# A graph layer by gathers: single rows given up for wider steps, and the waiting fillers computed by shifted sums and minima

## The chip, the cores and the metric

The kernel runs on one core of one Trainium2 chip. The metric is the device time of one execution in microseconds (us), as the median of several runs; lower is better. The engines of a core work side by side, each through its own list of instructions: PE multiplies matrices (its weight loads are shown apart, as PEld), DVE (VectorE) and ACT (ScalarE) work element by element, POOL (GpSimd) here does little else than issue gathers, and SP (SyncE) issues DMAs. A DMA moves data between memory and the core's on-chip buffers without any of them.

## The reference

N = 50000 nodes have D = 128 features each, and there are E = 1,650,000 edges (src, dst, type 0 or 1), sorted by dst. Every node has one edge to itself among them. The edges' messages are summed per destination, then a residual and a normalization follow:

```
msg = where(edge_type == 0, x[src] @ W_data.T + b_data, x[src] @ W_control.T + b_control)
agg = segment_sum(msg, dst)
out = layernorm(x + relu(agg + x @ W_self.T + b_self))
```

Since the message is linear in x[src], the kernel first sums the rows x[src] for each destination and type, and applies the two weight matrices to the sums. The heavy part is reading 1.6 million rows of 512 bytes at addresses that the data gives.

## The kernel before, in words

**Blocks and steps.** The sorted edges are cut into NBLK = 514 blocks of Q = 2 steps. A step has R = 12 columns of 128 edges, one edge in each of the 128 partitions, and in addition S = 24 edges that are fetched as single rows and F = 46 *fillers*, of which below. A block so takes up to 3212 edges in the order of their destinations and covers at most B = 112 destinations, a step at most W = 60. The first and the last block (`plain`) have neither single rows nor fillers; the last has RCH = 19 columns.

**Gathers.** For each column of 128 edges POOL issues one indirect DMA (L536) that fetches 128 rows of x into a tile `y`, by the addresses in `idx` (or `sdt`, the loaded list itself, for the last block, and `idx0` for the first). Gathers come in passes of PASS = 6, one tile `y` per pass; there are SLOTS = 10 such tiles, so POOL can be at most ten passes ahead of the products that read them. PE waits for a pass by a semaphore (L543).

**Products.** DVE compares each edge's column number (its destination relative to the step's first, plus W where the type is 1) with 0 to 2W - 1, which gives a one-hot matrix `oh` (L467), and counts the edges per destination (`cnt`, L475). For each column PE multiplies: the gathered rows as weights, the one-hot as the moving side, accumulated over the step in `acc` (L555); the single rows follow as one more product (L561), the counts as two (L564). In f32 each product shows as two loads and two matmuls in the trace. DVE adds a step's `acc` to the block's `sums` at the place of the step (`add`, L569). In the next block's turn PE applies the weights (`layer`, L586 to L590), DVE computes the residual and the moments (L596 to L603), ACT the root (L612), DVE the result (L618, L621), and SP stores it (L626).

**Single rows.** `offsets` (L490, DVE) turns source numbers into byte offsets, and `single_rows` (L496 to L513) has SP and ACT load them into registers and issue one DMA of 512 bytes for each, 12 per step on each of the two queues. PE waits for them in `rows_fetched` (L515 to L520).

**Self edges and fillers.** A node's edge to itself needs no gather, because x of the block's own nodes is there in any case (`window`, L438, by SP; `positions`, L453). Such an edge leaves a free place among the gathered columns, and a later edge, a *filler*, takes it. For each group of GB = 10 blocks, `columns` (L261) ranks the free places with matmuls (L284 to L287, `rank`), checks the order of the edges, packs source and column number into one number (L253), and follows, step by step, how many fillers are still waiting for a place: a chain of 20 additions with a lower bound of zero (L322 to L324, `late`), of which at most LATE = 10 may wait at once; FX = LATE + F. For each block, `spread` (L340, PE) puts the list of its fillers on all partitions, and `fill` (L349, DVE) finds the filler of each free place (L358 to L368), makes the gather's addresses `idx` (L369) and notes which self edge was left out (L373 to L378). `left_out_columns` (L384, PE), `left_out_matrix` (L392, DVE), `left_out_numbers` (L400, L403, PE) and `left_out_rows` (L409, DVE) make of it what is added to the sums instead (`begin_sums`, L571).

**Order.** The order is written by hand, and each engine keeps to it. One iteration of the loop (L682 to L735) is one block: loads for later blocks, `spread` for one or two later blocks (L690 lets the lists get up to RAHEAD = 5 blocks ahead, two blocks per iteration at most), the last `add` of the block before, `begin_sums`, `onehot` and `counts` two blocks ahead; then the four passes, with `fill` after the first, the layer of the block before after the second, `columns` of the next group after the third pass of the group's second block (L725), and the root and the stores after the fourth. Before the loop (L661 to L679) stand `columns(0)`, the lists of blocks 1 and 2 and the first one-hots. The block numbers that SP and DVE read as addresses (`base_i`, `at_i`) are computed ahead of `columns(0)` (L205 to L223). In the last block `find_bad` (L628) collects the checks; a kernel for general data (`general`) would run if they failed, and it doesn't with these data.

Of the kernel before, what the change touches and what calls it, by code (L numbers as in the profile page):

```python
# [21 lines left out]
ACT = mybir.EngineType.Activation  # L22
# [23 lines left out]
LOADS = 1  # L46
BEGIN = (0, -(-Q * TURNS[0] // 4) * 4)
X = BEGIN[1] + -(-Q * TURNS[1] // 4) * 4
R1 = R + 1
# [4 lines left out]
BE = CE + Q * (F + S)  # L54
# [27 lines left out]
GS = GB * Q  # L82
SPAN = 8
# [14 lines left out]
def straight(ctx, tc, c, x, x_t, edges_t, edges_f, src_x, dst_first, first_p, out):  # L98
# [62 lines left out]
    row_of = keep.tile([GB, GB], BF16, name="row_of")  # L161
    nc.vector.tensor_copy(row_of, c["ident"][:GB, :GB])
# [7 lines left out]
    one_g = {}  # L170

    def load_edges(g):
        t = eds.tile([1, GB * X], I32, name="one_g")
        nc.sync.dma_start(t, src_x[None, g * GB * X:(g + 1) * GB * X])
        one_g[g] = t
# [28 lines left out]
    nc.vector.tensor_tensor(begin_p, begin_p, base_p, op=ALU.add)  # L204
    wide = keep.tile([1, WG, SPAN], F32, name="wide")  # L205
    bases_f = keep.tile([1, WG * SPAN], F32, name="bases_f")
    nc.vector.memset(bases_f, float(N - B))
    nc.vector.tensor_copy(bases_f[:, :NBLK], base[0:1, :NBLK, 0])
    first_of_span = bases_f.rearrange("o (w s) -> o w s", s=SPAN)
    nc.vector.tensor_scalar(wide, first_of_span[:, :, 0:1].to_broadcast([1, WG, SPAN]), float(N - WIDE), None, op0=ALU.min)  # L210
    within = keep.tile([1, WG, SPAN], F32, name="within")
    nc.vector.tensor_tensor(within, first_of_span, wide, op=ALU.subtract)
    at_i = keep.tile([1, WG * SPAN, 4], I32, name="at_i")
    nc.vector.tensor_copy(at_i[:, :NBLK, :Q], begin[0:1, :NBLK, :])
    nc.vector.tensor_scalar(at_i[:, :, 3], within.rearrange("o w s -> o (w s)"), 0.0, float(WIDE - B), op0=ALU.max, op1=ALU.min)
    nc.vector.tensor_tensor(begin, begin, base.to_broadcast([P, BL, Q]), op=ALU.add)
    base_i = keep.tile([1, WG, 2 * SPAN], I32, name="base_i")
    nc.vector.tensor_scalar(base_i[:, :, 0], wide[:, :, 0], 4.0, None, op0=ALU.mult)
    nc.vector.tensor_scalar(base_i[:, :, 1:1 + SPAN], first_of_span, float(ROW), None, op0=ALU.mult)
    shift = keep.tile([1, NBLK], F32, name="shift")  # L220
    nc.vector.memset(shift, 0.0)
    nc.vector.tensor_tensor(shift[:, 1:], base[0:1, 1:NBLK, 0], base[0:1, :NBLK - 1, 0], op=ALU.subtract)
    nc.vector.tensor_scalar(at_i[:, :NBLK, 2], shift, 0.0, float(B), op0=ALU.max, op1=ALU.min)  # L223


# [27 lines left out]
    def packed(src, col):  # L253

        lim = eds.tile(list(col.shape), F32, name="lim", bufs=1)
        nc.vector.tensor_scalar(lim, col, 0.0, float(COLS - 1), op0=ALU.max, op1=ALU.min)
# [4 lines left out]
    def columns(g):  # L261
# [16 lines left out]
        h = eds.tile([P, GB, Q, R1], BF16, name="h_loop", bufs=1)  # L278
# [3 lines left out]
        rank = ps_r.tile([P, GB * Q, R1], F32, name="rank")  # L282
# [6 lines left out]
        col, rel = columns_of(a["d"], a["t"], first_of, "")  # L289
        check(a["d"], rel, [stats[:, 0, m, g:g + 1] for m in range(2)], "")  # L290
        col_f, rel_f = columns_of(a["df"], a["tf"], first_of_f, "_f")
# [5 lines left out]
        with nc.allow_low_precision(reason="whole numbers below 256 times a power of two"):  # L297
            nc.vector.tensor_scalar(v_f[:, 0, :], col_f, 0.0, float(COLS - 1), op0=ALU.max, op1=ALU.min)
            lo = eds.tile([GB, Q * FX], F32, name="lo", bufs=1)
# [30 lines left out]
        if n < GS and g > 0:  # L330
            nc.vector.memset(late[:, n + 1:], 0.0)
# [745 lines left out]
```

## Time and profile before

| what | us |
| --- | --- |
| median of 3 runs | 17994.12 |
| the 3 runs | 17983.56 to 17994.94 |
| the profiled execution | 18008.86 |
| its span (first to last instruction) | 18006.8 |
| mean granted TensorE clock, share of full speed | 0.54 |

The span is what the rows of the profile cover. A row of the page's fifth part, or of the view by lines, names a line of the kernel, the engine, the operation, the tiles out<-in with their shapes, the count, then after the bar the busy time in us, the mean of one in ns, and the idle time of the engine just before them with what ended most of it: an engine and its operation, "issue" when the engine waited for nothing that the profile shows, or "remote" for a releaser that the profile doesn't name. A row of the timeline gives the start, the duration, engine, line and operation, the count of equal instructions in a row, and in brackets the idle time before and its releaser. The table by stretches gives for a stretch of the span its length and each engine's busy time with its count in the order PE, PEld, DVE, ACT, POOL, then the granted clock, the mean busy share of the DMA engines and GB/s. The view of a line by source gives name, count and the shortest, middle and longest duration in ns.

### The profile page before, as it was taken

The page shows a single profiled execution, that of the slowest core. Times are in us where ns is not written, and L with a number is a line of the kernel's source. Part 1 is how long each engine was busy: PE and PEld are TensorE (multiplying, and loading weights), DVE is VectorE, ACT ScalarE, POOL GpSimd, SP SyncE. Part 2 cuts the span into 40 slices and gives each one's busy share as a digit, 9 for nine tenths or more (in the row PEclk, how much of TensorE's full clock was granted, in tenths as well). Part 3 has the DMA queues.
Part 4 walks back from the last instruction along what each step waited for, and adds up shares of the span by engine and source line. Part 5 has one row for each costly group of instructions (what it writes and reads, how often), then busy time and mean ns, then how long its engine had stood idle before and what let it go on. Part 6 is the DMA issues. An engine that isn't in the chain of part 4 may idle for free.

```text
span 18006.8 us, 165600 instructions
## 1 busy us (share of the span) xinstructions
PE 8608.7 (48%) x37659; PEld 7345.2 (41%) x37660; DVE 12374.8 (69%) x15212; ACT 79.2 (0%) x263; POOL 11686.9 (65%) x12341
## 2 busy tenths in 40 slices
PE   3444444444444444444444444444444444444444
PEld 3344443444344444444444444444444444444444
DVE  7676676676666666666766766676676676667665
ACT  0000000000000000000000000000000000000000
POOL 6666666666666666666666666666666666666666
PEclk6555555555555555555555555555555555555555
DMA  1111111111111111111111111111111111111111
GB/s 52 51 50 51 52 50 51 52 50 51 50 52 51 50 52 50 51 51 51 51 50 52 51 50 51 51 51 51 51 51 50 51 52 50 51 52 50 51 50 48
DMA packets 529272, 913.91 MB, mean 51 GB/s; under 512 B 232762, under 2 KB 315875, under 8 KB 528274
## 3 DMA queue, kind: packets, MB, share of 16 engines
q0 software_dynamic: 394592, 808.89, 15.7%
q1 hardware_dynamic: 108668, 87.80, 1.7%
q10 hardware_dynamic: 25014, 6.54, 0.2%
q8 instruction: 306, 5.01, 0.1%
q14 instruction: 692, 5.67, 0.1%
HBM read 872.82 MB, written 29.47 MB: 50 GB/s over the span
## 4 chain that ended last, share of the span: by engine, by line
DVE 51%; another core or an unknown queue 28%; issue 13%; PE 7%; DVEq 0%; ACTq 0%; ACT 0%
DVE cnt L475 14%; DVE oh L467 8%; PE acc L555 5%; DVE m L358 4%; DVE v_new L365 4%; DVE new L361 4%; DVE old L374 4%; DVE sums L569 2%; DVE late L323 1%; DVE z L392 1%; DVE h L597 1%; DVE st L599 1%; DVE xT L461 1%; DVE h L596 1%
## 5 line engine op out<-in xcount | busy, mean ns | idle before, releaser
L536 POOL DMA_INDIRECT y<-in_x,idx x12312 | 11667.4, 948 | 6272.6 <-issue 3435.2
L555 PEld LDWEIGHTS acc<-oh,y 128*128 128x128 f32 x24662 | 5375.0, 315 | 8665.3 <-issue 8100.0
L555 PE MATMUL acc<-oh,y 128*128 128x120 f32 x24662 | 6002.7, 413 | 3679.8 <-issue 3675.4
L569 DVE TENSOR_TENSOR sums<-acc,sums 128x180 f32 x1028 | 350.0, 340 | 4142.8 <-remote 3960.0
L475 DVE TENSOR_REDUCE cnt<-oh 128x240 bf16<-128x3120 f32 x514 | 3008.2, 5852 | 17.9
L384 PE MATMUL small<-ones_b,by 128*112 128x1 bf16 x512 | 83.5, 164 | 4632.6 <-issue 3934.5
L467 DVE TENSOR_TENSOR oh<-col,small 128x3120 f32<-128x3120 f32 x514 | 1740.8, 3387 | 117.3 <-remote 95.1
L377 DVE TENSOR_REDUCE by<-old 128x112 bf16<-128x1456 f32 x512 | 1427.3, 2788 | 17.4
L358 DVE TENSOR_TENSOR m<-rk,small 128x1456 f32<-128x1456 f32 x512 | 855.7, 1671 | 17.4
L361 DVE TENSOR_TENSOR new<-m,small 128x1456 f32<-128x1456 f32 x512 | 855.2, 1670 | 17.5
L365 DVE TENSOR_REDUCE v_new<-new 128x26 f32<-128x1456 f32 x512 | 855.0, 1670 | 17.5
L374 DVE TENSOR_TENSOR old<-m,small 128x1456 f32<-128x1456 f32 x512 | 852.5, 1665 | 0.0
L561 PE MATMUL acc<-oh,yx 24*128 24x120 f32 x2048 | 758.6, 466 | 61.6 <-issue 61.6
L590 PE MATMUL po<-wmsgT,sums 128*112 128x128 f32 x2056 | 612.8, 453 | 5.5 <-issue 5.5
L561 PEld LDWEIGHTS acc<-oh,yx 24*128 24x128 f32 x2048 | 486.9, 292 | 293.0 <-issue 281.7
L596 DVE COPY h<-po 112x128 f32<-112x128 f32 x514 | 144.8, 282 | 537.1 <-remote 451.3
L590 PEld LDWEIGHTS po<-wmsgT,sums 128*112 128x112 f32 x2056 | 448.4, 297 | 130.7 <-issue 130.0
L347 PE MATMUL small<-v_f,row_of 10*128 10x112 bf16 x1536 | 218.2, 272 | 563.8 <-DVE at L391 168.6
L588 PE MATMUL po<-bias,sums 3*112 3x128 f32 x1028 | 391.5, 482 | 0.2 <-DVE sums L569 0.2
L347 PEld LDWEIGHTS <-row_of 10*128 10x128 bf16 x1536 | 121.7, 112 | 599.5 <-issue 562.2
L587 PE MATMUL po<-wselfT,xT 128*112 128x128 f32 x1028 | 324.9, 420 | 0.0
L564 PE MATMUL acc<-cnt,to_row 128*128 128x60 bf16 x2056 | 281.2, 227 | 13.8 <-issue 13.7
(141 smaller groups left out, 4709.2 us busy)
## 6 DMA issues: line engine op xcount, KB each, us to landing
y<-in_x,idx POOLq DMA_INDIRECT x12312
yx<-in_x SPq DMA_DIRECT2D x12288, 0.5 KB
yx<-in_x ACTq DMA_DIRECT2D x12288, 0.5 KB
xw<-in_x_t SPq DMA_DIRECT2D x65, 448.0 KB
out<-o SPq DMA_DIRECT2D x514, 56.0 KB
sdt<-in_edges_t SPq DMA_DIRECT2D x52, 390.0 KB
one_g<-in_src_x SPq DMA_DIRECT2D x52, 1.9 KB
sdt_f<-in_edges_f SPq DMA_DIRECT2D x52, 13.1 KB
```

The lines of the kernel that those rows point to most:

```text
L358: nc.vector.tensor_tensor(m, rk_g[g][:, i, :, None].to_broadcast([P, C1, FX]), rank_no_ps[:, None, :].to_broadcast([P, C1, FX]), op=ALU.is ...
L361: nc.vector.tensor_tensor(new.rearrange("p (q r) f -> p q r f", r=R1), m.rearrange("p (q r) f -> p q r f", r=R1), vf.rearrange("p (q f) -> ...
L365: nc.vector.tensor_reduce(v, new, AX.X, ALU.add)
L374: nc.vector.tensor_tensor(old, m, cb[:, :, None].to_broadcast([P, C1, FX]), op=ALU.mult)
L377: nc.vector.tensor_reduce(by, old.rearrange("p (q r) f -> p q f r", r=R1), AX.X, ALU.add)
L467: nc.vector.tensor_tensor(oh, col_g[g][:, i, :, None].to_broadcast([P, C1, 2 * W]), num_ps[:, None, :].to_broadcast([P, C1, 2 * W]), op=AL ...
L475: nc.vector.tensor_reduce(cnt, ohs[b].rearrange("p (q r) w -> p q w r", r=R1), AX.X, ALU.add)
L536: copy = nc.gpsimd.indirect_dma_start(out=y[:r, k % PASS, :].bitcast(U8), out_offset=None, in_=x_rows, in_offset=bass.IndirectOffsetOnAxis ...
L555: nc.tensor.matmul(acc[:, :2, :].rearrange("p t w -> p (t w)"), y[:r, k % PASS, :], ohs[b][:r, column(k), :], start=k == of_step[0], stop= ...
L561: nc.tensor.matmul(acc[:, :2, :].rearrange("p t w -> p (t w)"), ys[b][:, q, :], ohs[b][:S, q * R1 + R, :], start=False, stop=True)
L569: nc.vector.tensor_tensor(part, accs.pop((b, q)), part, op=ALU.add)
L590: nc.tensor.matmul(po, a[:, t, :B], c["wmsgT"][:, t * D:(t + 1) * D], start=False, stop=t == 1)
```

## The change

Six things are changed together.

1. **No single rows.** `offsets`, `single_rows`, `rows_fetched`, their tiles, their semaphores and the product L561 go. In their place a step has R = 14 gathers instead of 12, in passes of 7 instead of 6, F = 53 fillers instead of 46, W = 64 and B = 124. A block takes up to 3690 edges; there are 448 of them, and the last has RCH = 6 columns. The number of tiles `y` (ten) stays.
2. **Waiting fillers** (L322 to L324): instead of the chain of 20 additions on single columns, five shifted additions over the whole group give the running sums, five shifted minima give the least of them so far, and the difference is the number that waits.
3. **Other forms on DVE**: in `columns` most operations with a tensor and two numbers (`tensor_scalar`) become operations with two tensors and a number (`scalar_tensor_tensor`); the test of the type is made once (`nz`) and used twice.
4. **One list per block at first**: an iteration makes at most one new list as long as b is at most GB // 2 = 5, and at most two from then on (two from the start before).
5. **Columns later**: `columns` of the next group stands after the third pass of a group's fifth block (i == 4) instead of its second.
6. **Start and end**: the block numbers are computed behind `fill(1)`, the one-hot of block 0 ahead of the left-out columns. `find_bad` comes one block earlier. The last block is taken out of the loop: its gathers come in passes of 2, the layer of the block before it stands ahead of them, its own part of the layer that needs no sums (`own_part`) too, and it is normalized and stored alone.

```diff
-R = 12
-W = 60
+R = 14
+W = 64
 Q = 2
-PASS = 6
-B = 112
+PASS = 7
+B = 124
 C = R * Q
-F = 46
+F = 53
 LATE = 10
 FX = LATE + F
-TURNS = (12, 12)
-S = sum(TURNS)
...
-R1 = R + 1
+R1 = R
+H = R + 1
...
-BE = CE + Q * (F + S)
+BE = CE + Q * F
...
+    def block_numbers():
+        nc.vector.memset(bases_f, float(N - B))
+        nc.vector.tensor_copy(bases_f[:, :NBLK], base[0:1, :NBLK, 0])
...
     def columns_of(d, t, first, name):
 
+        nz = eds.tile(list(d.shape), F32, name="nz" + name, bufs=1)
+        one = ones_f[:d.shape[0], :, None] if len(d.shape) == 3 else ones_f[:d.shape[0], :]
+        nc.vector.scalar_tensor_tensor(nz, t, 0.0, one.to_broadcast(list(d.shape)), op0=ALU.not_equal, op1=ALU.mult)
...
-        nc.vector.tensor_scalar(col, t, 0.0, float(W), op0=ALU.not_equal, op1=ALU.mult)
-        nc.vector.tensor_tensor(col, col, rel, op=ALU.add)
-        return col, rel
+        nc.vector.scalar_tensor_tensor(col, nz, float(W), rel, op0=ALU.mult, op1=ALU.add)
+        return col, rel, nz
...
-        more = eds.tile([P, GS], F32, name="more", bufs=1)
-        nc.vector.tensor_scalar(more, rank[:, :, R], -1.0, float(F), op0=ALU.mult, op1=ALU.add)
+        up, low = runs[:, :2], runs[:, 2:]
+        nc.vector.scalar_tensor_tensor(up[:, 0, PAD + 1:], rank[:, :, R], -1.0, fills_f.to_broadcast([P, GS]),
+                                       op0=ALU.mult, op1=ALU.add)
...
+        by, i = 1, 0
+        while by <= GS:
+            nc.vector.tensor_tensor(up[:, 1 - i, PAD:], up[:, i, PAD:], up[:, i, PAD - by:PAD + GS + 1 - by], op=ALU.add)
+            by, i = 2 * by, 1 - i
+        total = up[:, i, PAD:]
+        least, by, i = up[:, i, :], 1, 0
+        while by <= GS:
+            nc.vector.tensor_tensor(low[:, i, PAD:], least[:, PAD:], least[:, PAD - by:PAD + GS + 1 - by], op=ALU.min)
+            least, by, i = low[:, i, :], 2 * by, 1 - i
         late = eds.tile([P, GS + 1], F32, name="late")
...
-        for k in range(at, n):
-            nc.vector.tensor_scalar(late[:, k + 1:k + 2], more[:, k:k + 1], late[:, k:k + 1], 0.0,
-                                    op0=ALU.add, op1=ALU.max)
+        nc.vector.tensor_tensor(late, total, least[:, PAD:], op=ALU.subtract)
...
     def passes_of(b):
 
-        for p in range(C // PASS):
-            q = p * PASS // R
-            yield q, [k for k in chunks_of(b, q) if k // PASS == p]
+        of = 2 if b == NBLK - 1 else PASS
+        for p in range(C // of):
+            q = p * of // R
+            yield q, [k for k in chunks_of(b, q) if k // of == p]
...
         if ks[-1] == of_step[-1]:
-            if not plain(b):
-                if q == 0:
-                    rows_fetched(b)
-                nc.tensor.matmul(acc[:, :2, :].rearrange("p t w -> p (t w)"), ys[b][:, q, :],
-                                 ohs[b][:S, q * R1 + R, :], start=False, stop=True)
             for t in range(2):
...
-    for b in range(1, AHEAD + 1):
-        offsets(b)
     columns(0)
-    window(0)
     spread(1)
     fill(1)
+    block_numbers()
+    window(0)
+    onehot(0)
+    counts(0)
     left_out_columns(1)
...
-        due, fresh = fresh, range(made + 1, min(b + RAHEAD, made + 2, NBLK - 1) + 1)
+        due, fresh = fresh, range(made + 1, min(b + RAHEAD, made + (2 if b > GB // 2 else 1), NBLK - 1) + 1)
...
+        if b == NBLK - 1:
+            layer(b - 1)
+            moments(b - 1)
+            root(pair(b - 1))
+            own_part(b)
+            store(pair(b - 1))
+            for done in pair(b - 1):
+                store_rows(done)
+            for step, ks in passes_of(b):
+                if ks:
+                    products(b, step, ks)
...
+            break
...
-            if q == 2 and i == 1 and g + 1 < GROUPS:
+            if q == 2 and i == GB // 2 - 1 and g + 1 < GROUPS:
                 columns(g + 1)
...
-            if q < LOADS and not plain(b + AHEAD):
-                single_rows(b + AHEAD, q)
```

More of the change, by code (lines that the diff above doesn't have):

```diff
@@ L82 @@
 GS = GB * Q
+PAD = 16
 SPAN = 8
@@ L587, in layer @@
         nc.tensor.matmul(po, xT, c["wselfT"], start=True, stop=False)
+        pos[b] = both
+    def layer(b):
+        if b not in pos:
+            own_part(b)
+        a = sums[b % RING]
+        po = pos[b][:, 0, :]
         nc.tensor.matmul(po, a[0:3, 2, :B], bias, start=False, stop=False)
@@ L677, in straight @@
         counts(b)
-        for part in range(LOADS):
-            single_rows(b, part)
     made, fresh = 2, [2]
     ready = []
-    for b in range(NBLK + 1):
+    for b in range(NBLK):
+        if b == NBLK - 2:
+            find_bad()
         if b == NBLK - 1:
-            find_bad()
+            if pair(b - 2):
+                store(pair(b - 2))
+                ready.extend(pair(b - 2))
+            while ready:
+                store_rows(ready.pop(0))
         if b + 3 < NBLK:
@@ L735, in straight @@
                 store_rows(ready.pop(0))
-    store(pair(NBLK - 1))
-    for b in (*ready, *pair(NBLK - 1)):
-        store_rows(b)
+    b = NBLK - 1
+    add(b, steps_of(b)[-1])
+    layer(b)
+    moments(b)
+    root(pair(b))
+    store(pair(b))
+    store_rows(b)
 def general(ctx, tc, c, x, src, dst, etype, out):
@@ L1035 @@
         rest = a[CE:].reshape(TBL - 1, BE)
-        steps = rest.reshape(TBL - 1, Q, SIZE + S + F)
+        steps = rest.reshape(TBL - 1, Q, SIZE + F)
         cols = np.full((TBL, Q, R1, P), pad, np.int32)
```

170 lines of the change are left out of this document (62 added, 108 removed).

## The prediction

> **What bounds the kernel now.** I read the page first, for engine shares and the largest groups.
>
> ```profile
> span 18006.8 us, 165600 instructions
> ...
> PE 8608.7 (48%) x37659; PEld 7345.2 (41%) x37660; DVE 12374.8 (69%) x15212; ACT 79.2 (0%) x263; POOL 11686.9 (65%) x12341
> ...
> L536 POOL DMA_INDIRECT y<-in_x,idx x12312 | 11667.4, 948 | 6272.6 <-issue 3435.2
> ```
>
> No engine is full. POOL comes closest to a bound in the sense that matters: it issues every gather, and its idle time (6272.6 us) is short pieces before each gather and long pieces before some. So the second view is the table by stretches, for the steady part, where POOL's column has its time and its count.
>
> ```profile
> 200.00:17900.00 17700.00, 8500.00 (x37116) 7251.30 (x37115) 12168.79 (x14877) 74.72 (x253) 11515.70 (x12154) 0.54 0.18 51
> ```
>
> 17700 / 12154 = **1.456 us per gather**. The third view is POOL's timeline, which shows what this consists of. A typical train of gathers, and the longest one, near the start:
>
> ```profile
> 9041.73 0.95 POOL L536 DMA_INDIRECT y<-in_x,idx  x1 [2.93 <-remote]
> ...
> 9055.49 0.95 POOL L536 DMA_INDIRECT y<-in_x,idx  x1 [0.30 <-issue]
> 9059.25 0.95 POOL L536 DMA_INDIRECT y<-in_x,idx  x1 [2.81 <-DVE old L374]
> ```
>
> ```profile
> 33.80 0.95 POOL L536 DMA_INDIRECT y<-in_x,idx  x1 [0.30 <-issue]
> 46.20 0.95 POOL L536 DMA_INDIRECT y<-in_x,idx  x1 [11.45 <-DVE idx L369]
> ...
> 89.98 0.95 POOL L536 DMA_INDIRECT y<-in_x,idx  x1 [0.30 <-issue]
> 97.59 0.95 POOL L536 DMA_INDIRECT y<-in_x,idx  x1 [6.67 <-remote]
> ```
>
> The first train has 12 gathers (two passes), 11 steps in 13.76 us: 1.251 us each. Then the next start is 3.76 us away, 2.51 us more than a step. The second has 36 gathers and then 7.61 us, 6.36 us more. So the long wait grows with the train: (6.36 - 2.51) / 24 = 0.160 us per gather, and 0.59 us once per train. **Something is owed for each gather and paid back before POOL may go on.** What it is shows on the other engines. PE in the first of these fences' neighbourhood, just before:
>
> ```profile
> 9013.23 0.36 PE L555 MATMUL acc<-oh,y 128*128 128x120 f32 x1 [0.99 <-issue]
> ...
> 9023.74 3.28 PE L555 MATMUL acc<-oh,y 128*128 128x120 f32 x16 [1.74 <-issue]
> ```
>
> Between these stand three more matmuls, each with a weight load ahead: 8 instructions in 10.51 us, 1.31 us apiece, waiting for nothing but "issue", and then 16 in 3.28 us as soon as the train is paid off. PE is fed slowly while gathers run, quickly for a moment afterwards. And its results are seen late:
>
> ```profile
> 9027.36 0.23 PE L564 MATMUL acc<-cnt,to_row 128*128 128x60 bf16 x2
> ```
>
> ```profile
> 9041.57 0.35 DVE L569 TENSOR_TENSOR sums<-acc,sums 128x180 f32 x1 [13.99 <-remote]
> ```
>
> L569 adds what L564 finished; it starts 14 us later, 0.16 us before POOL's own restart at 9041.73. So in the steady part: POOL issues until its ten slots wait for PE; PE, DVE and POOL then move on together when the debt is paid. The period is 1.251 + 0.160 = 1.411 us per gather plus 0.59 us per train. From the stretch, (17700 - 12154 x 1.411) / 0.59 = 934 trains, 13.0 gathers each, 1.84 trains per block of 24.
>
> **The change part by part.**
>
> *Gathers.* Before: 513 blocks of 24 and one of 19, 12331 gathers. After, with 448 blocks, C = 28 and RCH = 6: 447 x 28 + 6 = 12522, 1.55% more, since the rows that SP and ACT fetched singly (24 per step) now lie in gathers. At the old mean that is 191 x 1.456 = +278 us. A gather stays 128 rows of 512 bytes, so I leave its 1.251 and 0.160.
>
> *Single rows.* SP and ACT lose 12288 DMAs each, with register loads; PE loses L561 (2 matmul and 2 load records per step, 8 per block) and the wait for those rows. Does this remove the debt? Late in the run the single rows are over before the gathers are:
>
> ```profile
> 17907.34 22.06 SPq L510 DMA_DIRECT2D yx<-in_x  x24
> ```
>
> ```profile
> 17900.51 21.93 ACTq L510 DMA_DIRECT2D yx<-in_x  x31
> ```
>
> ```profile
> 17937.18 0.36 PE L555 MATMUL acc<-oh,y 128*128 128x120 f32 x1 [1.04 <-issue]
> 17938.58 0.36 PE L555 MATMUL acc<-oh,y 128*128 128x120 f32 x1 [1.04 <-issue]
> 17939.98 0.36 PE L555 MATMUL acc<-oh,y 128*128 128x120 f32 x1 [1.04 <-issue]
> ```
>
> From 17929.4 nothing is issued on SP's or ACT's queue for single rows, and PE still crawls, one matmul and one load per 1.40 us, 0.70 us apiece. So **the gathers alone make the debt**; single rows only double PE's step, from 0.70 to 1.31 us. [...]
>
> *What the freed feed is worth.* PE and PEld together have 75319 records, 146.5 per block, 79.6 per train. A train and its wait last 24 x 1.411 / 1.84 + 0.59 = 19.0 us; at 1.31 us apiece the crawl gives 14.5 of them, so a fast spell gives about 65. After, a block needs 146.5 - 8 + 4 x 4 = 154.5 records. With d trains per block: 65 + (39.5 / d + 0.59) / step = 154.5 / d. A step of 0.70 us gives d = 1.49, 1.31 us gives 1.90. DVE goes on fetching, so I take the middle, **d = 1.68**, and keep both ends. A block then costs 28 x 1.411 + 1.68 x 0.59 = 40.50 us (40.39 to 40.63).
>
> *DVE.* Wider one-hots (28 x 128 instead of 26 x 120) and fillers (28 x 63 instead of 26 x 56):
>
> ```profile
> L475 DVE TENSOR_REDUCE cnt<-oh 128x240 bf16<-128x3120 f32 x514 | 3008.2, 5852 | 17.9
> L384 PE MATMUL small<-ones_b,by 128*112 128x1 bf16 x512 | 83.5, 164 | 4632.6 <-issue 3934.5
> L467 DVE TENSOR_TENSOR oh<-col,small 128x3120 f32<-128x3120 f32 x514 | 1740.8, 3387 | 117.3 <-remote 95.1
> L377 DVE TENSOR_REDUCE by<-old 128x112 bf16<-128x1456 f32 x512 | 1427.3, 2788 | 17.4
> L358 DVE TENSOR_TENSOR m<-rk,small 128x1456 f32<-128x1456 f32 x512 | 855.7, 1671 | 17.4
> L361 DVE TENSOR_TENSOR new<-m,small 128x1456 f32<-128x1456 f32 x512 | 855.2, 1670 | 17.5
> L365 DVE TENSOR_REDUCE v_new<-new 128x26 f32<-128x1456 f32 x512 | 855.0, 1670 | 17.5
> L374 DVE TENSOR_TENSOR old<-m,small 128x1456 f32<-128x1456 f32 x512 | 852.5, 1665 | 0.0
> ```
>
> 9.24 us x 1.149 + 9.46 us x 1.212 = 22.1 us; with the other 24.1 - 18.7 = 5.4 us that is 27.5 us per block of 40.5, 68% as now. It waits instead:
>
> ```profile
> DVE sums L569 <- remote: 3960.0, 513, 20.4
> ```
>
> That is 7.7 us per block. It hides the rest of DVE's edits at nothing: the chain of 20 additions for waiting fillers, which becomes ten shifted sums and minima, the extra nz, and the columns moved from the second to the fifth block of a group. Without this cover each would cost its own time, a few us per group of ten blocks.
>
> *Fewer plain scalar operations.* [...]
>
> ```profile
> L536 POOL DMA_INDIRECT y<-in_x,idx x12312: 939/947/2020, 3.0 to 17941.2; - x199
> ```
>
> The mean is 948 ns and the median 947: 12 us in all are to be had here. I count none.
>
> *Start and end.* The second block's first gather stands at 46.20, held by DVE. With the block numbers later and one list at a time, POOL's own 28 gathers bind: 33.80 + 4 x 1.25 + 1.25 = 40 us (40 to 46). Behind the last gather:
>
> ```profile
> 17968.54 0.95 POOL L536 DMA_INDIRECT y<-in_x,sdt  x1 [0.30 <-issue]
> ```
>
> ```profile
> 17984.10 5.45 PE L555 MATMUL acc<-oh,y 128*128 128x120 f32 x24
> ```
>
> 38.3 us to the end of the span. The last block falls from 19 gathers to 6, 13 x 2 records at 5.45 / 24 = 5.9 us, and the find_bad work and one store go earlier; I take 31 us (28 to 38).
>
> *Sum.* 40 + 446 x 40.50 + 8.5 (six gathers) + 31 = 18143 us of span, against 18006.8. The profiled execution took 18008.86 us, 2.1 us more than its span and 14.7 us above the median of the three runs, 17994.12. In terms of that median: 18143 + 2 - 15 = **18130 us**, 0.76% slower. With the ends of d, start and end: 18080 to 18200; since the two trains fix 0.160 and 0.59 to some hundredths only, 18030 to 18250.
>
> **The rivals.**
>
> 1. *The debt goes with the single rows.* Then POOL issues a gather every 1.251 us and never waits: 40 + 12494 x 1.251 + 31 = 15700 us. [...] Against it: the crawl after 17929, and the train of 36, most of it without single rows, whose wait fits the same line. It decides as soon as the debt per gather falls below zero, that is 0.160 us must be theirs. 0.14. A part of it would do for a gain: 0.02 us less per gather is 250 us.
>
> 2. *PE is fed so much better that a block needs one train only*, four passes: 446 x (39.51 + 0.59) = 17885, in all 17950 us. For it: the step of 0.70. Against it: PE waits in every block at L384 for a one-hot that waits for L569, which is released by the end of a train; and 154.5 records are more than 65 + 57. 0.14, half of it within 0.2%.
>
> 3. *More trains*: PE's fast spell doesn't reach over two passes of seven with the layer between them, 14 x 4 + 30 records, so trains of 7 mix in. At d = 2.6, 446 x 41.04 = 18305, in all 18370 us. For it: 86 records are more than 65 + 14. Against it: now the same two passes take 80. 0.12.
>
> **How the numbers follow.** Forecast 0.60, all of it slower; rival 1 0.14, faster; rival 2 0.14 (0.06 faster, 0.08 same); rival 3 0.12, slower. About 0.2% (17958 to 18030) is what a measurement of this kernel can tell from no change. Faster 0.20, same 0.08, slower 0.72. The range 17930 to 18310 holds the forecast, most of the second rival and the lower part of the third; the first, and the upper third, are left out with 0.2.
>
> **What would show it.** In the new profile's stretch, POOL at 1.43 to 1.46 us per gather; trains of 14 and 21 gathers at 1.251 us with waits of 2.8 and 4.0 us beyond a step; single matmuls 0.7 to 1.3 us from their loads while SP and ACT rest; the second block's first gather near 40 us and some 31 us behind the last one. I am wrong if the long waits are gone or no longer grow with the train (rival 1), if trains of 28 prevail (2), or if they are mostly of 7 (3).

## The result, and the profile after

The kernel after took **17875.78 us** (median of four runs, 17872.18 to 17878.55) beside 17990.78 us for the kernel before in the same comparison (four runs, 17983.56 to 17994.94). The ratio is 0.9939, 95% interval 0.9928 to 0.9951: 0.6% faster. The forecast was 18130 us, 0.76% slower, with a range that began at 17930. The profiled execution of the kernel after took 17875.51 us, 1.7 us more than its span.

The page of the kernel after, the lines that answer to those shown of before:

```profile
span 17873.8 us, 103324 instructions
...
PE 6946.3 (39%) x34670; PEld 6006.5 (34%) x34671; DVE 11876.6 (66%) x12324; ACT 69.8 (0%) x231; POOL 11880.6 (66%) x12532
...
L499 POOL DMA_INDIRECT y<-in_x,idx x12516 | 11873.2, 949 | 5958.3 <-issue 3574.2
...
L390 PE MATMUL small<-ones_b,by 128*126 128x1 bf16 x446 | 72.6, 163 | 1917.8 <-DVE oh L474 1352.2
```

Over a third of the instructions is gone, 62276 of 165600. PE's busy time falls by 1662 us, which buys nothing by itself. What counts is POOL's idle time: 314.3 us less, although POOL issues 191 more gathers. PE's idle time ahead of the left-out columns (L384 before, L390 now) falls from 4632.6 us, 9.0 per block, to 1917.8, 4.3 per block.

The table by stretches of the kernel after, columns as for before:

```profile
200.00:17700.00 17500.00, 6819.72 (x34025) 5898.77 (x34025) 11666.61 (x12048) 64.66 (x219) 11651.03 (x12284) 0.60 0.20 51
```

17500 / 12284 = **1.425 us per gather**, where before had 1.456 and the forecast 1.446 (40.50 / 28). DVE's 11666.61 us are 26.6 per block of 28 gathers; forecast 27.5. POOL's timeline of the kernel after, two restarts in a row with nothing but back-to-back gathers between them:

```profile
9099.20 0.95 POOL L499 DMA_INDIRECT y<-in_x,idx  x1 [5.02 <-PE acc L522]
...
9132.96 0.95 POOL L499 DMA_INDIRECT y<-in_x,idx  x1 [0.30 <-issue]
9139.04 0.95 POOL L499 DMA_INDIRECT y<-in_x,idx  x1 [5.13 <-PE small L353]
```

39.84 us from restart to restart are 27 steps in 33.76 us, 1.250 each, and a last one of 6.08: **a train of 28 gathers, one whole block**, then 4.83 us beyond a step. Counted over both timelines of POOL from 200 us on (a new train begins where a gather starts over 1.8 us after the one before it):

| | before | after |
| --- | --- | --- |
| gathers in all | 12331 | 12522 |
| trains, from 200 us on | 917 | 462 |
| trains per block | 1.81 | 1.04 |
| commonest trains | 12 (456 times), 18 (310) | 28 (407) |
| their middle wait beyond a step, us | 2.53, 3.46 | 4.82 |
| all long waits beyond a step, whole span, us | 2512 | 2147 |
| last gather to the end of the span, us | 38.3 | 31.3 |

The difference of the spans is -133.0 us: 191 gathers more at 1.252 us are +239, the waits -365, the end -7. The waits give more than the gathers cost.

POOL's long waits were not there in every comparison, so each ratio below stands against the kernel before of its own comparison, and "with pauses" or "without pauses" says which it met.

### The profile page after: what moved, and what is told of

Its sections match the earlier page's. It is cut to its first block, busy times and chain, and to the rows that moved or that the text cites. A ratio compares the mean times of both kernels' runs of the same rounds, so it can differ in the third digit from the quotient of the medians.

```text
span 17873.8 us, 103324 instructions
## 1 busy us (share of the span) xinstructions
PE 6946.3 (39%) x34670; PEld 6006.5 (34%) x34671; DVE 11876.6 (66%) x12324; ACT 69.8 (0%) x231; POOL 11880.6 (66%) x12532
## 4 chain that ended last, share of the span: by engine, by line
DVE 51%; another core or an unknown queue 27%; issue 17%; PE 5%; DVEq 0%; DMA 0%; ACT 0%; ACTq 0%
DVE cnt L482 14%; DVE oh L474 9%; DVE m L364 4%; DVE v_new L371 4%; DVE new L367 4%; DVE old L380 4%; PE acc L518 4%; DVE sums L527 2%; DVE sums L538 1%; DVE z L398 1%; DVE st L562 1%; DVE h L560 1%; DVE xT L468 1%; DVE h L559 0%
## 5 line engine op out<-in xcount | busy, mean ns | idle before, releaser
L518 PE MATMUL acc<-oh,y 128*128 128x128 f32 x25044 | 5433.2, 373 | 4761.1 <-issue 4725.3
L518 PEld LDWEIGHTS acc<-oh,y 128*128 128x128 f32 x25044 | 4793.6, 277 | 7175.2 <-issue 5937.1
L482 DVE TENSOR_REDUCE cnt<-oh 128x256 bf16<-128x3584 f32 x448 | 2807.1, 6266 | 15.4
L474 DVE TENSOR_TENSOR oh<-col,small 128x3584 f32<-128x3584 f32 x448 | 1737.4, 3878 | 255.4 <-remote 185.4
L383 DVE TENSOR_REDUCE by<-old 128x126 bf16<-128x1764 f32 x446 | 1466.5, 3288 | 15.5
L364 DVE TENSOR_TENSOR m<-rk,small 128x1764 f32<-128x1764 f32 x446 | 888.5, 1992 | 17.7 <-remote 1.7
L367 DVE TENSOR_TENSOR new<-m,small 128x1764 f32<-128x1764 f32 x446 | 888.1, 1991 | 15.2
L371 DVE TENSOR_REDUCE v_new<-new 128x28 f32<-128x1764 f32 x446 | 887.9, 1991 | 15.2
L380 DVE TENSOR_TENSOR old<-m,small 128x1764 f32<-128x1764 f32 x446 | 884.8, 1984 | 0.0
L390 PE MATMUL small<-ones_b,by 128*126 128x1 bf16 x446 | 72.6, 163 | 1917.8 <-DVE oh L474 1352.2
L554 PE MATMUL po<-wmsgT,sums 128*124 128x128 f32 x1792 | 428.5, 367 | 82.5 <-issue 79.7
```

Source lines behind the costliest of these rows:

```text
L364: nc.vector.tensor_tensor(m, rk_g[g][:, i, :, None].to_broadcast([P, C1, FX]), rank_no_ps[:, None, :].to_broadcast([P, C1, FX]), op=ALU.is ...
L367: nc.vector.tensor_tensor(new.rearrange("p (q r) f -> p q r f", r=R1), m.rearrange("p (q r) f -> p q r f", r=R1), vf.rearrange("p (q f) -> ...
L371: nc.vector.tensor_reduce(v, new, AX.X, ALU.add)
L380: nc.vector.tensor_tensor(old, m, cb[:, :, None].to_broadcast([P, C1, FX]), op=ALU.mult)
L383: nc.vector.tensor_reduce(by, old.rearrange("p (q r) f -> p q f r", r=R1), AX.X, ALU.add)
L474: nc.vector.tensor_tensor(oh, col_g[g][:, i, :, None].to_broadcast([P, C1, 2 * W]), num_ps[:, None, :].to_broadcast([P, C1, 2 * W]), op=AL ...
```

## The experiments

**Two conditions.** With pauses, as in the result, the kernel before took 17881 to 18074 us; without pauses 15464 to 15494 us. All kernels of one comparison met the same condition. It is not the chip: three chips were met in both. The number of trains per block, on which the prediction failed, exists only with pauses.

The theories: **A**, the single rows' load on the other engines broke the block into 1.8 trains, and their going made it one. **B**, the new sizes or the new order did. Later A splits: **A1**, the instructions and DMAs of SP and ACT; **A2**, PE's wait for the rows and its product of them. **C**, the wait behind a train is a debt of the gathers, whatever PE has to do; **D**, POOL waits only because a starved PE gives its slots back late.

**The kernel after itself, without pauses.**

> The kernel after itself, unchanged. In the first four runs POOL never paused and the kernel before took 15465 us, so this shows which of two chips' behaviours these comparisons meet. Where POOL pauses after each train, as in the first result: 17876 us and 0.994 of the kernel before. Where it never pauses: only the count of gathers and the ends matter, 12522 x 1.2495 + 31 + 3 = 15680 us, 1.014 of the kernel before.

Measured: 15682.18 us beside 15463.85, ratio 1.0141 (1.0124 to 1.0158). The same change that gains 0.6% with pauses costs 1.4% without them. The page:

```profile
span 15680.6 us, 103324 instructions
...
L499 POOL DMA_INDIRECT y<-in_x,idx x12516 | 11843.1, 946 | 3815.1 <-issue 3734.4
L518 PE MATMUL acc<-oh,y 128*128 128x128 f32 x25044 | 5944.0, 430 | 8061.7 <-PEq L506 8061.7
...
L527 DVE TENSOR_TENSOR sums<-acc,sums 128x192 f32 x895 | 315.2, 352 | 3436.1 <-PE acc L522 3436.1
```

POOL's idle time is the 0.30 us between gathers and hardly more (0.305 in the mean); PE waits for gathers (L506 is its wait for a pass), not POOL for PE. Here the time is the count of gathers: the first starts at 3.3 us, 12521 steps of 1.251 us in the mean follow, and the span ends 13.8 us behind the last, 15680 us in all. The 191 gathers more are 239 us, of which 218 show. The start and the end give some 20 back: in a trace without pauses of a kernel that keeps the order of before (e12_b_one_dma), 17 us of waits lie in the first 150 us, and the last gather stands 18.4 us ahead of the end; the kernel after has no such wait, and 13.8.

**The kernel before without its single rows.**

```diff
-                             start=k == of_step[0], stop=plain(b) and k == of_step[-1])
+                             start=k == of_step[0], stop=k == of_step[-1])
...
-            if not plain(b):
-                if q == 0:
-                    rows_fetched(b)
-                nc.tensor.matmul(acc[:, :2, :].rearrange("p t w -> p (t w)"), ys[b][:, q, :],
-                                 ohs[b][:S, q * R1 + R, :], start=False, stop=True)
...
-            single_rows(b, part)
...
-            if q < LOADS and not plain(b + AHEAD):
-                single_rows(b + AHEAD, q)
```

> The kernel before without its single rows: SP and ACT issue none, the product that reads them (L561) and PE's wait for them are gone; the 48 edges per block that came singly are left out of the sums, everything else (12 gathers per step, passes of 6, the order, the lists, DVE's work) stays. Theory A (the single rows' load on PE's feed kept the block at two trains): one train of 24 per block, its wait 4.5 us, so about 513 x (24 x 1.252 + 4.5) + 70 = 17790 us or a little less. Theory B (the new sizes or the new order brought the one train): trains of 12 and 18 stay, within 0.2% of the kernel before, 17990 us.

Without pauses: 15455.08 us, ratio 0.9993 (0.9984 to 1.0003). It tells nothing of trains; single rows cost nothing there that can be measured.

> The kernel before without its single rows, as in the first of these experiments (the 48 edges per block that came singly are left out of the sums, the order and all sizes stay), for a chip on which POOL pauses. Theory A, the single rows' going: about one train of 24 per block, 513 x (24 x 1.252 + 4.1 to 4.5) + 75 = 17590 to 17800 us, ratio 0.985 to 0.995. Theory B, the new order and forms on DVE: trains of 12 and 18 stay, 1.8 per block, ratio 0.998 to 1.002. On a chip where POOL never pauses: 0.9993 again.

With pauses: 17559.06 us beside 17880.98, ratio **0.9819** (0.9802 to 0.9835), faster still than I had put for theory A. POOL's timeline of this run:

```profile
9071.48 0.95 POOL L536 DMA_INDIRECT y<-in_x,idx  x1 [5.19 <-remote]
...
9100.25 0.95 POOL L536 DMA_INDIRECT y<-in_x,idx  x1 [0.30 <-issue]
9105.54 0.95 POOL L536 DMA_INDIRECT y<-in_x,idx  x1 [4.34 <-remote]
```

28.77 us from the first row to the second are 23 steps: 24 gathers, one block, and 5.29 us to the next. Of 548 trains 458 are of 24; 1.08 per block. The old order, sizes and DVE work are all there, so theory A holds and B is not needed.

**The new order with the old sizes.**

```diff
-R = 14
-W = 64
+R = 12
+W = 60
...
-PASS = 7
-B = 124
+PASS = 6
+B = 112
...
-F = 53
+F = 46
```

> The kernel after with the sizes of the kernel before: R = 12, W = 60, PASS = 6, B = 112, F = 46, no single rows; 521 x 24 + 13 = 12517 gathers, five fewer than the kernel after. Where POOL pauses: theory A (the single rows' going made one train per block) gives one train of 24 with a wait of 4.5 us, 519 x (24 x 1.252 + 4.5) + 80 = 18010 us; theory B (the sizes did it) gives 1.8 trains again, 519 x (24 x 1.411 + 1.8 x 0.59) + 80 = 18200 us. Where POOL never pauses, the count alone decides: 12517 x 1.2495 + 35 = 15675 us.

With pauses: 17814.35 us beside 17890.9, ratio 0.9958 (0.9942 to 0.9975). It lies below both of my numbers: 399 of 601 trains are of 24, 1.17 per block, as A has it, but with a middle wait of 4.05 us, shorter than the 4.5 that I had put in, and the kernel before was 100 us faster in this comparison too. Wider steps would be worth only the difference to 0.9939 of the kernel after, about 0.2%; the two intervals overlap, so even that isn't shown.

**Which part of the single rows.** One DMA of 24 rows per block on each queue replaces 24 single ones; PE's wait and product stay.

```diff
-        for pair in zip_longest(*both):
-            for dma, sem, q, k, at, row in filter(None, pair):
-                copy = dma.dma_start(ys[b][at + k:at + k + 1, q, :].bitcast(U8), x_bytes[:, bass.ds(row, ROW)])
...
+        for j, dma in enumerate((nc.sync, nc.scalar)):
+            n, at = TURNS[j], sum(TURNS[:j])
+            copy = dma.dma_start(ys[b][at:at + n, :, :], x[j * Q * n:(j + 1) * Q * n, :].rearrange("(q k) d -> k q d", q=Q))
```

> The kernel before with one DMA of 24 rows per block on each of the two queues in place of 24 single DMAs with their register moves; the rows come from fixed addresses, so the sums hold wrong rows; PE's wait for them, their product and DVE's offsets stay. Theory A1 (the 100 instructions per block of SP and ACT crowd the others): like the kernel without single rows, one train of 24, 0.980 to 0.985. Theory A2 (PE's wait for the rows and its product of them break the block in two): 1.8 trains stay, 0.998 to 1.002. On a chip without pauses: 1.000.

> As in the run of this kernel before it (one DMA of 24 rows per block on each queue in place of 24 single DMAs with register moves; wrong rows in the sums), for a chip on which POOL pauses. Theory A1 (SP's and ACT's 100 instructions per block crowd the others): one train of 24, 0.980 to 0.985 of the kernel before. Theory A2 (PE's wait for the rows and its product of them break the block in two): 1.8 trains stay, 0.998 to 1.002.

> Once more one DMA of 24 rows per block on each queue in place of 24 single DMAs (wrong rows in the sums), for a condition in which POOL pauses. Theory A1 (SP's and ACT's 100 instructions per block crowd the others): one train of 24, 0.980 to 0.985 of the kernel before. Theory A2 (PE's wait and its product of them break the block in two): 1.8 trains stay, 0.998 to 1.002. Where POOL never pauses: 1.000.

Without pauses: 0.9999 (0.9989 to 1.0008), 0.9998 (0.9988 to 1.0008) and 0.9999 (0.9988 to 1.0011). It tells nothing there.

> The kernel before with one DMA of 24 rows per block on each queue in place of 24 single DMAs (wrong rows in the sums), for a condition in which POOL pauses. Theory A1 (SP's and ACT's 100 instructions per block crowd the others): one train of 24, 0.980 to 0.985 of the kernel before. Theory A2 (PE's wait and its product of them break the block in two): 1.8 trains stay, 0.998 to 1.002. Where POOL never pauses: 1.000.

With pauses, in two runs: 17733.51 us beside 18074.32, ratio **0.9811** (0.9783 to 0.984). POOL's timeline:

```profile
9065.86 0.95 POOL L528 DMA_INDIRECT y<-in_x,idx  x1 [4.72 <-remote]
...
9094.72 0.95 POOL L528 DMA_INDIRECT y<-in_x,idx  x1 [0.30 <-issue]
9100.34 1.10 POOL L528 DMA_INDIRECT y<-in_x,idx  x1 [4.68 <-remote]
```

Again 24 gathers in a train, 1.06 trains per block, and the same gain as without any single row. A1 holds; PE's wait and product cost nothing that can be measured. Whether it is the instructions themselves or the 48 small transfers that they start, these runs don't separate. The pages' rows of ACT's queue, the kernel before first, then this run:

```profile
q10 hardware_dynamic: 25014, 6.54, 0.2%
```

```profile
q10 hardware_dynamic: 18870, 6.51, 0.1%
```

Without any single row (the run of ratio 0.9819) that queue has 438 packets. So the kernel before has 24576 packets there for 12288 single rows, one of 512 bytes and one of 4 each, and this run 18432 for 512 DMAs of 24 rows, by the packets' sizes 24 of 512 bytes and 12 of 4 each. What in a single row it is that breaks a train, no run here shows.

**How much of it a block bears.** Half and five quarters of the single rows, all edges kept.

```diff
-TURNS = (12, 12)
+TURNS = (6, 6)
```

> The kernel before with half its single rows: 6 instead of 12 per step on each of the two queues, all edges kept, 517 x 24 + 16 = 12424 gathers (93 more than before, 98 fewer than after). Where POOL pauses: if half of SP's and ACT's instructions leave room for one train per block, 518 x (24 x 1.252 + 4.2) + 75 = 17815 us of a kernel before at 17990, ratio 0.988 to 0.992, better than both kernels; if the block still breaks, 1.4 to 1.8 trains, 1.000 to 1.008. Where POOL never pauses, the count alone: 1.0075.

With pauses: 17979.66 us beside 18010.49, ratio 0.9982 (0.9972 to 0.9991), 1.53 trains per block. The trains are those of my second case, the time lies between the two: it works by degrees, and it is no better than the kernel after.

```diff
-TURNS = (12, 12)
+TURNS = (15, 15)
```

> The kernel before with 15 instead of 12 single rows per step on each of the two queues: 12286 gathers instead of 12331. Where POOL never pauses: 45 x 1.2495 = 56 us less than the kernel before, ratio 0.9964, if SP and ACT can issue 30 rows in the 30 us of a block; if they can't, PE waits for the rows and the time rises to 30 x 1.0 us per block or more. Where POOL pauses: theory A gives more trains and a slower kernel than before, theory B 45 x 1.456 = 65 us less.

With pauses: 17890.58 us beside 17890.9, ratio 1.000 (0.999 to 1.001). The trains rise to 1.97 per block, as A has it, but they only eat what 45 fewer gathers save; the kernel isn't slower than before, as I had put for A. So 0, 24, 48 and 60 single rows per block go with 1.08, 1.53, 1.81 and 1.97 trains.

**Single rows put back into the kernel after.** The functions of before, fed with the first 24 entries of the block's `idx`; PE waits for them and multiplies them.

```diff
+            if q == 0 and not plain(b + AHEAD):
...
+                single_rows(b + AHEAD)
...
+                nc.tensor.matmul(acc[:, :2, :].rearrange("p t w -> p (t w)"), ys[b][:, q, :],
+                                 ohs[b][:S, q * R1 + R - 1, :], start=False, stop=True)
```

> The kernel after with single rows put back beside its 14 gathers: 12 by SP and 12 by ACT per step, at the place in the order that they had, PE's wait for them and one product per step of them; these rows are extra, so the sums hold rows that do not belong. Theory A: the block falls back to about 1.8 trains, 446 x (28 x 1.411 + 1.8 x 0.59) + 71 = 18160 us. Theory B: one train of 28 stays, 17880 to 17900 us.

> The kernel after with single rows put back beside its 14 gathers (24 per step, extra rows that do not belong in the sums), for a chip on which POOL pauses. Theory A: the block of 28 falls back from one train to about 1.8, and the time to 446 x (28 x 1.411 + 1.8 x 0.59) + 71 = 18160 us, 1.005 to 1.015 of the kernel before. If the sizes protect the rhythm: one train of 28 and 0.994. On a chip without pauses: 1.0133 again.

Both met no pauses: 1.0133 (1.0116 to 1.015) and 1.0131 (1.0114 to 1.0148), the kernel after's own ratio there but for 0.1%.

> The kernel after with 24 single rows per step put back beside its 14 gathers (extra rows that do not belong in the sums), for a condition in which POOL pauses. Theory A: the block of 28 falls back from one train to about 1.8, 1.005 to 1.015 of the kernel before. If the sizes protect the rhythm: one train of 28 and 0.994. Where POOL never pauses: 1.013.

With pauses, in two runs: 18242.87 us beside 18050.19, ratio **1.0107** (1.0077 to 1.0136). POOL's timeline of this run:

```profile
9110.56 0.95 POOL L535 DMA_INDIRECT y<-in_x,idx  x1 [4.22 <-remote]
...
9131.07 0.95 POOL L535 DMA_INDIRECT y<-in_x,idx  x1 [3.25 <-remote]
...
9151.50 0.94 POOL L535 DMA_INDIRECT y<-in_x,idx  x1 [3.22 <-remote]
```

20.5 us from restart to restart: trains of 14, half a block. 855 trains, 1.93 per block. The sizes protect nothing. And 1.0107 is near what the prediction had for the kernel after, 18130 / 17994 = 1.0076: **the forecast's sum was about that of a kernel that has kept its single rows.** PE's idle time at the left-out columns is back as well:

```profile
L390 PE MATMUL small<-ones_b,by 128*126 128x1 bf16 x446 | 72.6, 163 | 3940.3 <-DVE oh L474 3382.9 <-issue 557.5
```

8.8 us per block, as before the change.

**Is the wait a debt, or PE's lateness?** One product per pass of gathers instead of seven.

```diff
         for k in ks:
+            if k not in (of_step[0], of_step[-1]):
+                continue
```

> The kernel after with one product per pass of gathers instead of seven (the first and the last column of a step alone; the other columns' rows are fetched and left out of the sums). PE has 96 records less per block, all else stays. Theory C (POOL waits because gathers leave a debt that is paid back by a pause, whatever PE has to do): the waits stay at 4.8 us per 28 gathers, 17880 us. Theory D (POOL waits only for slots that a starved PE gives back late): no long waits, 12522 x 1.252 + 70 = 15750 us. Between the two if PE still needs more than its fast spell.

> The kernel after with one product per pass of gathers instead of seven (the other columns' rows are fetched and left out of the sums), for a chip on which POOL pauses. PE has 96 records less per block. Theory C (gathers leave a debt that only a pause pays back, whatever PE has to do): a wait of 4 to 5 us per 28 gathers stays, 17750 to 17880 us, 0.993 of the kernel before. Theory D (POOL waits only for slots that a starved PE gives back late): few or no waits, down to 15700 us. On a chip without pauses: 15680 us again.

> As in the runs of this kernel before it (one product per pass instead of seven), for a chip on which POOL pauses. Theory C (gathers leave a debt that only a pause pays back, whatever PE has to do): a wait of 4 to 5 us per 28 gathers stays, 17750 to 17880 us, 0.993 of the kernel before. Theory D (POOL waits only for slots that a starved PE gives back late): few or no waits, down to 15700 us, 0.88.

Without pauses: 1.0138 (1.0121 to 1.0155), 1.0137 (1.012 to 1.0154) and 1.0137 (1.012 to 1.0154), what the count of gathers gives.

> The kernel after with one product per pass of gathers instead of seven (the other columns' rows are fetched and left out of the sums), for a condition in which POOL pauses. Theory C (gathers leave a debt that only a pause pays back, whatever PE has to do): a wait of 4 to 5 us per 28 gathers stays, 0.993 of the kernel before. Theory D (POOL waits only for slots that a starved PE gives back late): few or no waits, down to 15700 us, 0.87 to 0.88. Where POOL never pauses: 1.014.

With pauses, in two runs: 17705.8 us beside 18050.19, ratio 0.9809 (0.9781 to 0.9837). POOL's timeline:

```profile
9013.25 0.94 POOL L499 DMA_INDIRECT y<-in_x,idx  x1 [5.17 <-remote]
...
9081.89 0.94 POOL L499 DMA_INDIRECT y<-in_x,idx  x1 [0.30 <-issue]
9092.10 0.94 POOL L499 DMA_INDIRECT y<-in_x,idx  x1 [9.27 <-remote]
```

A train of 56 gathers, two blocks, and then 10.21 us, 8.96 beyond a step: 0.160 us for each of the 56. PE has nearly two thirds of its records less (25818 in the stretch from 200 to 17500 us, beside 68050 in 200 to 17700 for the kernel after), yet all waits together from 200 us on are 2002 us for 12378 gathers, 0.162 each, where the kernel after has 0.172. Trains of 56 are the commonest (107 of 316). The wait no longer goes with its own train: 75 trains of 14 have a middle wait of 7.03 us, 31 of 70 one of 3.00. Only the sum stays. C holds: the pause is owed, and a lighter PE pays it in fewer instalments. My number for C was too slow by 1.2%, in part because I had left the trains at 28.

The slots do come back late here too, but not because PE is busy. The layer of a block in this run, DVE's first reading of it, and PE's own next work:

```profile
9060.23 1.21 PE L556 MATMUL po<-wmsgT,sums 128*124 128x128 f32 x4
...
9090.38 0.29 DVE L561 COPY h<-po 124x128 f32<-124x128 f32 x1 [13.97 <-remote]
...
9091.63 0.47 PE L353 MATMUL small<-v_f,row_of 10*128 10x126 bf16 x3 [28.70 <-DVE at L397]
```

PE is done at 9061.44, DVE stands idle for 13.97 us and yet starts 28.94 us later, and PE waits 28.70 us for DVE. Nor is it the rows that are late. The table by stretches of the kernel after, its train of 28 shown above and the end of the wait behind it, where the last two columns are the DMA engines' share and GB/s:

```profile
9099.20:9136.00 36.80, 16.21 (x77) 14.20 (x77) 26.58 (x30) 0.29 (x1) 26.48 (x28) 0.59 0.21 54
9136.00:9139.00 3.00, 0.59 (x3) 0.24 (x2) 0.33 (x2) 0.00 (x0) 0.00 (x0) 0.50 0.00 0
```

Over all its trains the last packet of rows ends 2.2 us behind the start of the last gather, and POOL starts again 3.85 us later (both in the middle).

**DVE's edits undone.** The old chain of 20 additions, two lists per block from the start, and the columns at the second block, in the kernel after:

```diff
-        up, low = runs[:, :2], runs[:, 2:]
...
+        for k in range(at, n):
+            nc.vector.tensor_scalar(late[:, k + 1:k + 2], more[:, k:k + 1], late[:, k:k + 1], 0.0,
+                                    op0=ALU.add, op1=ALU.max)
...
-            if q == 2 and i == GB // 2 - 1 and g + 1 < GROUPS:
+            if q == 2 and i == 1 and g + 1 < GROUPS:
```

> The kernel after with three of its edits on DVE's side undone: the chain of 20 additions for waiting fillers, two lists per block from the start, and the next group's columns after the third pass of the second block instead of the fifth. Theory A (and the prediction, which counted these at nothing): within 0.2% of the kernel after, 17870 to 17900 us, and one train of 28 per block. Theory B with the order as its cause: trains of 14 and 21 come back in the blocks around the columns, 17950 us and more.

Without pauses: 15685.06 us beside 15464.92, ratio 1.0142 (1.0125 to 1.0159), the kernel after's own 1.0141. These edits are worth nothing there; with pauses they were not run alone.

**A version better than both** did not come out. With pauses nothing that keeps all edges beat the kernel after's 0.9939; without pauses the kernel before has fewer gathers than any kernel here that keeps all edges and about one train per block with pauses. The kernel with 15 single rows per queue and step has fewer still, 12286, and met no comparison without pauses.

## Why the prediction was wrong, by its own steps

- **What bounds the kernel: right.** POOL's steps of 1.249 to 1.252 us and the debt stand in every run with pauses. Over the nine kernels traced there, all waits per gather run from 0.162 (39.0 gathers per train) through 0.172 (26.8) to 0.203 (13.3). 0.145 us per gather and 0.75 per train, fitted to them, describe them within 0.012; the prediction had 0.160 and 0.59 from two trains.
- **Gathers: right.** 191 more, 239 us of issuing; in the condition without pauses they are nearly the whole difference.
- **"The gathers alone make the debt": right, where there is a debt.** With no single row at all the waits were 0.168 us per gather, with one product per pass 0.162; without pauses the same gathers leave none.
- **"What the freed feed is worth", d = 1.68: the step that failed.** The trace of the kernel after has d = 1.04. The step took the 1.31 us of one stretch for PE's pace through a whole train, 14.5 slow records, and what was left of a train's 79.6, 65, for a fixed store; then it kept the 65 and shortened the slow step to 0.70 us. Count over the whole traces, from 200 us on, a record of PE or PEld as slow when it starts 0.6 to 3 us after the one before, and as fast when it starts sooner. A train then holds 4.8 slow and 76 fast records before, and 14.4 and 133 after; the mean slow step is 1.14 us before and 1.12 after, and steps of about 0.70 and about 1.40 us stand in both. So the slow step has hardly changed, and there is no store of 65. The middle between 0.70 and 1.31 us took for granted that DVE's fetching slows PE, which no trace shows. Per block the fast records are the same, 137 and 139: they are a result of the rhythm, not its cause.
- **The price of a train and of a gather, taken as unchanged: together too dear.** With d = 1.04 the prediction's own sum, 446 x (28 x 1.411 + 1.04 x 0.59) + 79.5, gives 17974 us of span. That is 169 of the 269 us by which its 18143 was too long. The other 100 are the debt: with 0.145 and 0.75 in place of 0.160 and 0.59 it is 446 x (28 x 1.397 + 1.04 x 0.75) + 79.5 = 17873 (these two numbers are fitted afterwards). So d alone would have made the forecast 0.2% faster, not 0.6%.
- **Rival 2, one train per block, came true**, at 17876 where it was priced 17950, and its sign, that trains of 28 prevail, did too. What spoke against it, that PE waits in every block at L384 for a one-hot released at a train's end, still holds in the trace after (L390), but the wait now falls in the same train as the rest of the block. That 154.5 records were more than 65 + 57 rested on the same wrong store.
- **Rival 1, no debt at all, 15700 us:** the time was met, 15682 us, but not by this change: the kernel before has no debt there either. The chance of 0.14 was for the wrong cause.
- **DVE, start, end: right.** 26.6 us per block for 27.5; second block's first gather at 39.82 for 40, 31.3 us behind the last gather for 31. The row of the start:

```profile
39.82 1.04 POOL L499 DMA_INDIRECT y<-in_x,idx  x1 [0.30 <-issue]
```

- **Fewer plain scalar operations: right to count none.** No run shows that a gather's time depends on the form of DVE's operations; the 12 us are only the 1 ns between mean and median, times 12312 gathers. POOL's mean is 949 ns, before 948.

What stays open: how SP's and ACT's single DMAs break a train. That they do is shown by leaving them out, putting them back, halving them and replacing them; PE's slow step is much the same, 1.14 us in the kernel before and 1.12 without them. And what decides whether there are pauses at all.

## What to carry to other kernels

When an engine's rhythm is one long wait per batch, ask first how many batches the work falls into. A store and a rate that were read at one place of the trace (65 records, 1.31 us) were not those of the whole trace (76 records, 1.14 us); the kernel before without its single rows shows the batches directly. Small DMAs by other queues can cost an engine that never touches them: here the 48 single DMAs per block of SP and ACT cost the kernel before 1.8%, though PE, DVE and POOL were idle three tenths of the time or more, and only in one of two conditions. A gain of half a per cent should be tried in more than one session: this change has both signs.

## What the runs showed of the hardware that was not expected

**The same kernel, 15464 or 17991 us.** Without pauses PE's results reach DVE at once. Timeline of the kernel after there, the counts of a block's last step and the addition that waits for them:

```profile
9045.86 0.31 PE L522 MATMUL acc<-cnt,to_row 128*128 128x64 bf16 x2
...
9046.21 0.36 DVE L527 TENSOR_TENSOR sums<-acc,sums 128x192 f32 x1 [8.70 <-PE acc L522]
```

The addition starts 0.04 us after the counts end. With pauses the middle distance of this pair is 12.1 us in the kernel before and 21.7 in the kernel after. The page's part on DMAs differs too: without pauses the gathers of the kernel after have a time to landing, 2.5 us; with pauses its line has none.

```profile
y<-in_x,idx POOLq DMA_INDIRECT x12516, 2.5
```

```profile
y<-in_x,idx POOLq DMA_INDIRECT x12516
```

(The first of these is the kernel after without pauses, the second the profile of the result.) The single line is no sure sign: with single rows put back, without pauses (ratio 1.0133), it has no time either. The count of records of landings is: for the 12522 gathers of the kernel after the trace without pauses holds 200322, 16.0 per gather, the profile of the result 31813, 2.5 per gather. It is so in all: of 16 per gather the eleven traces without pauses hold 99.7% or more, the nine with pauses 13% to 19%. So one rival stays open: that the recording of the trace makes the pauses, and with them the gain of 0.6%. The other reading, that one cause makes POOL wait and the records go missing, fits as well. What delays a result while gathers are under way in one session and not in another, no run here shows.

**A pause of 0.16 us per gather that no engine's work explains.** It was nearly the same with PE at four tenths of its records (0.162 beside 0.172), and it let trains of 56 run before it was paid. The DMA engines moved nothing (0 GB/s) from 9136 to 9139 us, the last 3 us of the wait shown above.
